# Five-layer graph network: later, pinned maxima over two blocks' totals, an earlier end of the early sums, and a reordered last tile

## The chip, the cores and the metric

The kernel runs on one core of one Trainium2 chip. The metric is the device time of one execution in microseconds (us); lower is better.

## The reference

A block with a normalised input and a graph network over N = 6250 nodes and E = 100000 edges, sorted by destination. The destinations are skewed: low node numbers have many edges.

```python
h = jnp.maximum(_layernorm(x, axis=-1), 0.0)           # x: 6250 x 256
h = _sage_mean(h, src, dst, n, deg, W1_self, W1_neigh, b1)            # 512 wide
h = _sage_pool(h, src, dst, n, deg, W2_pool, b2_pool, W2_self, W2_neigh, b2)
h = _sage_gcn(h, src, dst, n, deg, W3_neigh, b3)
h = _sage_mean(h, src, dst, n, deg, W4_self, W4_neigh, b4)
return x + (h @ W_fc + b_fc)

def _sage_pool(h, src, dst, n, deg, W_pool, b_pool, W_self, W_neigh, b):
    hp = jax.nn.relu(h @ W_pool + b_pool)
    hmax = jax.ops.segment_max(hp[src], dst, num_segments=n)
    hmax = jnp.where(deg[:, None] > 0, hmax, 0.0)
    return h @ W_self + hmax @ W_neigh + b
```

`_sage_mean` takes the mean over the incoming edges instead of the maximum, `_sage_gcn` a sum with the node itself divided by the degree plus one. The change lies in the second layer, the one with the maximum.

## The kernel before

Nodes are cut into 49 tiles of 128. Layer 1 ends with `hp` in DRAM (`tab_p`, the head of `rows2`) and the transposed inputs of each tile in `tab_t`. Layer 3 begins with the table `tab_r`, which layer 2 writes tile by tile, as three bf16 pieces of a float32 value.

**Layer 2's walk.** The edges are cut into six blocks of 52, 100, 220, 180, 130 and 100 steps (782 in all; a step is 128 edges, one for each partition), walked from the last block to the first. Each step issues one indirect gather on GpSimd (L1574) of 128 rows of `hp` into a row tile `X` (six tiles of two steps each), and the vector engine keeps a running maximum along each partition's edges with `step` (L1555), three instructions for two steps. Every second step the running rows go back to DRAM (L1559) into the block's own region of `rows2`. When a block is through, `carry` handles runs that go on from one partition to the next: four transposes (L1361), scans (L1369) and products (L1373), transposes back (L1391 or L1379), a maximum with the stored row (L1394), and a store.

**The tiles.** A tile's maximum is then one gathered row of one block ("total", tile `tot`, L1450), or of two blocks if its edges lie on both sides of a boundary. Tiles 37, 36, 24, 23, 11, 10 and 1 have two totals, tile 0 has its own routine, and the others one. `done2(d)` is a generator that issues the totals' gathers and the load of `th`, lets some steps pass (`yield`), takes the maximum of two totals (L1465), transposes it (L1469, L1472), multiplies (L1476, L1479 and L1482, float32), and rounds the result into three bf16 pieces (L1490 to L1498, each piece subtracted from the sum again by a product with minus the identity). At most one tile is begun every 11 steps (7 in the first block), from the highest to the lowest. `last_done2(0)` does the same for tile 0 after the last carry. The pool for `tot` and `th2` has four buffers of each.

**The early sums.** Part of layer 3 is done ahead: for the 16 destination tiles with the most edges, `early_products` multiplies blocks of the edge-count matrix (`ae`, loaded at L1526) with the rounded pieces of tiles 6 to 37, in batches of four source tiles (L562 and L564, 12 bf16 products or a few more for each destination tile and batch, into one of two PSUM banks `pd`), and `add3` adds each result to an accumulator on the vector engine (L1286). A batch is recorded when its last tile is rounded. `early.advance` (L1611) paces the recorded work.

**Order.** The program records instructions in this order, and a planner then sorts each engine's queue by its own costs and due times, within the dependencies. What is wrapped in `tc.keep_in_program_order` keeps its place among the so marked instructions. On the chip each queue runs in the planned order.

Of the kernel before, what the change touches and what calls it, by code (L numbers as in the profile page):

```python
# [15 lines left out]
ALU = mybir.AluOpType  # L16
# [4 lines left out]
P = 128  # L21
# [56 lines left out]
def fast_path(  # L78
# [15 lines left out]
    nc = tc.nc  # L94
# [8 lines left out]
    T = (E + P - 1) // P  # L103
    EP = T * P
    KI = FI // P
# [98 lines left out]
    ident = const.tile([P, P], F32, name="identf")  # L204
# [30 lines left out]
    at = 0  # L235
# [1055 lines left out]
    with tc.tile_pool(name="fl2c", bufs=1) as ck, ExitStack() as late:  # L1291
# [5 lines left out]
        usA = ck.tile([P, KI, FH], F32, name="usA")  # L1297
# [112 lines left out]
        def last_done2(d):  # L1410
            tots = [total(d, b) for b in range(1, b_of[d][1] + 1)]
            th = wk.tile([P, 2 * KI, P], F32, name="th2", bufs=4)
            nc.scalar.dma_start(th, tab_t[d].rearrange("p (k n) -> p k n", n=P))
            while not carried:
                yield
            tots.append(total(d, 0))
            pc = bank(psm, "pm", "pc_last")
            nc.tensor.matmul(pc, takes[d], carried[0], start=True, stop=True)
            pm = bank(psb, "pb", "pm_last")
            for k in range(2 * KI):  # L1420
                us = usA[:, k, :] if k < KI else usB[:, k - KI, :]
                product = nc.tensor.matmul(pm, th[:, k, :], us, start=(k == 0), stop=False)
                if k == 0:
                    tc.keep_in_program_order(product)
            hm = tots[0]
            nc.vector.tensor_tensor(hm, hm, pc, op=ALU.max)
            for t in tots[1:]:
                nc.vector.tensor_tensor(hm, hm, t, op=ALU.max)
            pt = bank(pst, "pt", "pt_hTf", (KH, P))
            for j in range(KH):  # L1430
                nc.tensor.transpose(pt[:, j, :], hm[:, j * P : (j + 1) * P], ident)
            hT = wk.tile([P, KH, P], F32, name="hTf")
            nc.scalar.copy(hT, pt)
            for c in range(KH):
                nc.tensor.matmul(pm, hT[:, c, :], un[:, c, :], start=False, stop=(c == KH - 1))
            r3 = early_pool[0].tile([P, 3 * FH], BF16, name="r3", bufs=2 * BATCH + 1)
            for part in range(3):
                piece = r3[:, part * FH : (part + 1) * FH]
                nc.scalar.copy(piece, pm)
                if part < 2:  # L1440
                    nc.tensor.matmul(pm, minus_b, piece, start=False, stop=True,
                                     skip_group_check=True)
            nc.scalar.dma_start(tab_r[d * P : (d + 1) * P, :], r3)
            yield
# [13 lines left out]

        def done2(d):
            tots, th = totals(d)  # L1460
            for _ in range(6):
                yield
            hm = tots[0]
            for t in tots[1:]:
                nc.vector.tensor_tensor(hm, hm, t, op=ALU.max)  # L1465
            yield
            pt = bank(pst, "pt", "pt_hTf", (KH, P))
            for j in range(KH):
                nc.tensor.transpose(pt[:, j, :], hm[:, j * P : (j + 1) * P], ident)  # L1469
            yield  # L1470
            hT = wk.tile([P, KH, P], F32, name="hTf")
            nc.scalar.copy(hT, pt)  # L1472
            yield
            pm = bank(psm, "pm", "pm_prf")
            for k in range(KI):
                nc.tensor.matmul(pm, th[:, k, :], usA[:, k, :], start=(k == 0), stop=False)  # L1476
            yield
            for k in range(KI):
                nc.tensor.matmul(pm, th[:, KI + k, :], usB[:, k, :], start=False, stop=False)  # L1479
            yield  # L1480
            for c in range(KH):
                nc.tensor.matmul(pm, hT[:, c, :], un[:, c, :], start=False, stop=(c == KH - 1))  # L1482
                if c == 1:
                    yield
            yield
            yield
            yield
            r3 = early_pool[0].tile([P, 3 * FH], BF16, name="r3", bufs=2 * BATCH + 1)
            hi, mid, lo = (r3[:, i * FH : (i + 1) * FH] for i in range(3))
            nc.scalar.copy(hi, pm)  # L1490
            yield
            nc.tensor.matmul(pm, minus_b, hi, start=False, stop=True, skip_group_check=True)
            yield
            nc.scalar.copy(mid, pm)
            yield
            nc.tensor.matmul(pm, minus_b, mid, start=False, stop=True, skip_group_check=True)
            yield
            nc.scalar.copy(lo, pm)  # L1498
            nc.scalar.dma_start(tab_r[d * P : (d + 1) * P, :], r3)
            if EARLY[0] <= d < EARLY[1]:  # L1500
                ready.append((d, r3))
                if len(ready) == BATCH or d == EARLY[0]:
                    early_products()
            yield
# [61 lines left out]
        for b in reversed(range(NB)):  # L1566
# [3 lines left out]
            for s0 in range(0, tb, G2):  # L1570
                X = (xmore if at // G2 % 2 else xpool).tile([P, G2, FH], F32, name="X2")
                for k in range(G2):
                    t = t0 + s0 + k
                    nc.gpsimd.indirect_dma_start(  # L1574
                        out=X[:, k, :], out_offset=None, in_=tab_p,
                        in_offset=bass.IndirectOffsetOnAxis(ap=srcI[:, t : t + 1], axis=0),
                    )
                    row, st = X[:, k, :], same[:, t : t + 1]
                    if s0 + G2 >= tb:
                        step(row, X[:, 0, :] if k else run, st, row)  # L1580
                        if k:
                            stored(b, s0 // 2, X)
                    elif k == 0 and s0:
                        step(run, run, st, row)
                    elif k:
                        held = run if s0 else X[:, 0, :]
                        if s0 == 0:
                            step(run, held, st, row)
                        step(X[:, 0, :], row, st, held)
                        if s0:  # L1590
                            step(run, run, st, row)
                        stored(b, s0 // 2, X[:, :1, :])
                    at += 1
                    if at > 8:
                        next(steps, None)
                        if todo and next(todo[0], 0) == 0:
                            todo.pop(0)
                    if at >= 130 and at % 12 == 0:
                        next(finding, None)
                    if at == MADE_AT:  # L1600
                        for _ in steps:
                            pass
                        top.close()
                        early_pool.append(
                            top.enter_context(tc.tile_pool(name="early3", bufs=1)))
                    if at <= EARLY_AT:
                        hub.advance(math.ceil(len(first) * max(0, at - 16) / (EARLY_AT - 16)))
                    else:
                        hub.advance(len(first) + math.ceil(
                            len(rest) * (at - EARLY_AT) / (T - 100 - EARLY_AT)))  # L1610
                    early.advance(early.done + math.ceil(  # L1611
                        early.left() / max(1, min(32, T - 16 - at))))
                    if b == 0 and s0 == 0 and k == 0:
                        for _ in finding:
                            pass
                    if b == 0 and not tiles and not ends and last_tiles and at >= T - 14:
                        now += [last_done2(d) for d in last_tiles]
                        last_tiles.clear()
                    if s0 + k > 2 and ends and next(ends[0], 0) == 0:
                        ends.pop(0)  # L1620
                        tiles += [d for d in reversed(range(NT)) if b_of[d][0] == last_b]
                    if (tiles and not (b and ends) and at >= begun_at + (11 if b else 7)
                            and begun2 < NT * (at - FIRST_AT) / (T - 36 - FIRST_AT)):
                        begun_at = at
                        now.append(done2(tiles.pop(0)))
                        begun2 += 1
                    for g in list(now):
                        if next(g, 0) == 0:
                            now.remove(g)
# [788 lines left out]
```

## Time and profile before

| | |
|---|---|
| median of 3 runs | 2730.45 us (2728.73 to 2737.01) |
| profiled execution | 2726.43 us, span 2724.6 us |
| mean granted TensorE clock | 0.944 |
| PE, DVE, ACT, POOL busy | 87%, 76%, 33%, 71% of the span |
| first and last gather of layer 2's walk | 721.4 us, 1815.2 us |

Times in the views are microseconds from the span's start. A group row has the line, engine, operation, tiles and shapes, the count, then the busy time and the mean of one in ns, then the engine's idle time ahead of these instructions and what ended it. A timeline row has the start, the length, the engine, the line, and in brackets the idle time ahead of it and its releaser. PE is TensorE's matmuls, PEld its weight loads, DVE the vector engine, ACT the scalar engine, POOL GpSimd, SP the queue of direct DMAs. The share of busy time is an average over stages that differ; the change is in the stage from 727 to some 1848 us.

### The profile page before, as it was taken

The numbers are of one execution on the slowest core, as the hardware profiler recorded it, in microseconds if no ns is written. First come the engines' busy times: TensorE is split into PE (matmuls) and PEld (weight loads), VectorE is DVE, ScalarE is ACT, GpSimd is POOL, SyncE is SP. The second block draws the span as 40 slices with busy tenths as digits, with TensorE's granted clock in tenths as the row PEclk, the third lists the DMA queues.
The fourth block names the chain that finished last, engine by engine and source line by source line (L and its number), as shares of the span: only waits on it lengthen the run. The fifth ranks groups of instructions, "written<-read, shape, count | busy, mean of one in ns | idle before, by whom it ended". The sixth has DMA issues, their size and how long they took to land.

```text
span 2724.6 us, 39212 instructions
## 1 busy us (share of the span) xinstructions
PE 2368.6 (87%) x11542; PEld 1282.5 (47%) x11674; DVE 2076.7 (76%) x5555; ACT 904.5 (33%) x2190; POOL 1938.3 (71%) x2266
## 2 busy tenths in 40 slices
PE   4698999999786675989899939986999999999998
PEld 2356667677443332434344414442444444565554
DVE  8898777766699798889789988972767766466665
ACT  5567767764388777212111111110000101000000
POOL 6477777777577777777677777745777775677776
PEclk8799999999897887999899969998999999999999
DMA  9467677777799999999999999979999998888886
GB/s 288 150 185 206 206 211 216 217 230 221 245 377 354 337 362 362 345 359 352 312 351 356 348 336 344 348 243 351 379 378 393 386 363 309 248 239 240 238 247 200
DMA packets 352251, 805.91 MB, mean 296 GB/s; under 512 B 56174, under 2 KB 150870, under 8 KB 351996
## 3 DMA queue, kind: packets, MB, share of 16 engines
q0 software_dynamic: 146080, 513.79, 57.3%
q1 hardware_dynamic: 139368, 206.78, 20.9%
q10 hardware_dynamic: 66580, 82.73, 8.9%
q8 instruction: 95, 1.56, 0.2%
q14 instruction: 128, 1.05, 0.1%
HBM read 604.99 MB, written 198.91 MB: 295 GB/s over the span
## 4 chain that ended last, share of the span: by engine, by line
PE 47%; DMA 28%; DVE 12%; issue 6%; POOL 3%; ACT 1%; ACTq 0%; SPq 0%; DVEq 0%; another core or an unknown queue 0%; POOLq 0%
PE pd L564 12%; PE pg L505 11%; DMA X<-rows,srcIf 11%; DVE run L1555 5%; PE pd L556 4%; DMA rows<-X 4%; DMA ring<-tab_h,srcT 4%; PE pm_hp L1157 3%; DVE X L1555 3%; DMA ring<-tab_s,srcE 2%; PE pd L557 2%; POOL X L1574 2%; PE pm_hp L1154 2%; PE pb L346 2%; PE pg L500 2%
## 5 line engine op out<-in xcount | busy, mean ns | idle before, releaser
L1574 POOL DMA_INDIRECT X<-rows,srcIf x782 | 742.5, 950 | 276.3 <-issue 146.4
L1555 DVE SCALAR_TENSOR_TENSOR run<-run,samef,X 128x512 f32<-128x512 f32 x758 | 571.0, 753 | 42.3 <-DMA X<-rows,srcIf 37.1
L483 POOL DMA_INDIRECT ring<-tab_h,srcT x474 | 456.3, 963 | 148.9 <-issue 56.4
L505 PE MATMUL pg<-ring,hot 128*128 128x259 bf16 (+1 forms) x2432 | 512.1, 320 | 53.2 <-DMA ring<-tab_h,srcT 30.7
L534 DVE SCALAR_TENSOR_TENSOR acc<-pg,M,acc 128x256 f32<-128x256 f32 (+2 forms) x694 | 356.3, 538 | 106.0 <-PE pg L505 76.8
L483 POOL DMA_INDIRECT ring<-tab_r,srcE x342 | 331.7, 970 | 133.5 <-issue 54.9
L564 PE MATMUL pd<-r,ae 128*128 128x512 bf16 x1492 | 372.6, 385 | 32.9 <-DVE acc L1286 30.3
L483 POOL DMA_INDIRECT ring<-tab_s,srcE x314 | 299.4, 954 | 117.5 <-PE pg L501 38.6
L505 PEld LDWEIGHTS <-hot 128*128 128x128 bf16 x2448 | 239.6, 98 | 257.8 <-issue 98.3
L1555 DVE SCALAR_TENSOR_TENSOR X<-X,samef,run 128x512 f32<-128x512 f32 x379 | 281.4, 742 | 43.0 <-DMA X<-rows,srcIf 13.1
L556 PE MATMUL pd<-zt,ac 128*128 128x512 bf16 x835 | 291.0, 382 | 7.1 <-DMA ac<-tab_a 5.5
L564 PEld LDWEIGHTS <-ae 128*128 128x128 fp8e4 x1536 | 151.6, 99 | 250.3 <-issue 110.1
L479 DVE TENSOR_SCALAR hot<-iota_bf,keyE 128x128 bf16<-128x128 bf16 x656 | 159.3, 267 | 115.1 <-PE pg L505 82.0
L557 PE MATMUL pd<-zt,ac 128*128 128x256 bf16 x882 | 241.6, 274 | 2.7 <-DVE zt L312 0.2
L564 PE MATMUL pd<-zt,ac 128*128 128x512 bf16 x797 | 221.8, 380 | 0.9
L1482 PE MATMUL pm_prf<-unf,hTf 128*128 128x512 f32 x384 | 187.8, 615 | 5.6 <-ACT hTf L1472 5.4
L564 PE MATMUL pd<-Z,A 128*128 128x256 bf16 (+1 forms) x1176 | 184.4, 274 | 0.7 <-ACT A L351 0.6
L338 ACT ACTIVATE hs<-ht,onef 128x128 bf16<-128x128 bf16 x396 | 153.4, 393 | 90.2 <-PE pb L346 88.6
L346 PE MATMUL pb<-hm,hs 128*128 128x392 bf16 x461 | 146.3, 337 | 11.7 <-DVE hm L340 11.5
L337 ACT ACTIVATE ht<-iota_bf,sk 128x128 bf16<-128x128 bf16 x396 | 153.0, 398 | 8.3
L340 DVE TENSOR_SCALAR hm<-iota_w,mk 128x392 bf16<-128x392 f16 x461 | 149.7, 332 | 5.2 <-PE pb L346 4.7
L479 DVE TENSOR_SCALAR hot<-iota_bf,keyT 128x128 bf16<-128x128 bf16 x474 | 122.5, 267 | 40.6 <-PE pg L505 39.4
(381 smaller groups left out, 3498.9 us busy)
## 6 DMA issues: line engine op xcount, KB each, us to landing
rows<-X SPq DMA_DIRECT2D x385, 256.0 KB
tab_r<-r ACTq DMA_DIRECT2D x49, 384.0 KB
rows<-hpf SPq DMA_DIRECT2D x49, 256.0 KB
th<-tab_t ACTq DMA_DIRECT2D x49, 256.0 KB
X<-rows,srcIf POOLq DMA_INDIRECT x782
ac<-tab_a ACTq DMA_DIRECT2D x90, 112.0 KB
tab_t<-th SPq DMA_DIRECT2D x37, 256.0 KB
tab_h<-Z SPq DMA_DIRECT2D x16, 579.0 KB
```

Of the source, the lines that this page charges most:

```text
L338: nc.scalar.activation(hots[0], t, AF.Relu, bias=one, scale=-1.0)
L346: nc.tensor.matmul(hold[0], hots[0], hots[1], start=(k == 0), stop=(k == k_of[w] - 1))
L479: nc.vector.tensor_scalar(hot[j], iota_b, keyT[:, j - jb : j - jb + 1], None, op0=ALU.is_equal)
L483: nc.gpsimd.indirect_dma_start(out=ring[:, j % deep, :], out_offset=None, in_=table, in_offset=bass.IndirectOffsetOnAxis(ap=srcT[:, j - jb ...
L505: nc.tensor.matmul(pg[:, : F + c], hot[j], X[:, part * F : (part + 1) * F + c], start=(k == 0 and part == 2), stop=(k == n - 1 and part == 1),
L534: nc.vector.scalar_tensor_tensor(acc[d], half, m, acc[d], op0=ALU.mult, op1=ALU.add)
L556: nc.tensor.matmul(hold[0], a, z[:, : 2 * F], start=(s == ss[0]), stop=False)
L557: nc.tensor.matmul(hold[0][:, :F], a, z[:, 2 * F :], start=False, stop=(s == ss[-1]))
L564: nc.tensor.matmul(hold[0][:, : F + c], a, z[:, part * F : (part + 1) * F + c], start=(s == ss[0] and part == 2 and s != own), stop=(s == ...
L1482: nc.tensor.matmul(pm, hT[:, c, :], un[:, c, :], start=False, stop=(c == KH - 1))
L1555: nc.vector.scalar_tensor_tensor(put, held, st, row, op0=ALU.mult, op1=ALU.max)
L1574: nc.gpsimd.indirect_dma_start(out=X[:, k, :], out_offset=None, in_=tab_p, in_offset=bass.IndirectOffsetOnAxis(ap=srcI[:, t : t + 1], axis=0),
```

## The change

- In `done2`, a tile with two totals lets 11 steps pass instead of 6 before its maximum, and the maximum keeps its place in program order among the marked instructions.
- The deadline towards which the early sums are paced is 30 steps ahead of the walk's end instead of 16 (the divisor is at most 32, so it counts from step 720 on).
- In `last_done2`, the two products with `usB` come behind the transposes and the copy of the maximum instead of ahead of them, and these products and transposes keep their program order.

No instruction is added or removed.

```diff
@@ last_done2
             pm = bank(psb, "pb", "pm_last")
-            for k in range(2 * KI):
-                us = usA[:, k, :] if k < KI else usB[:, k - KI, :]
-                product = nc.tensor.matmul(pm, th[:, k, :], us, start=(k == 0), stop=False)
-                if k == 0:
-                    tc.keep_in_program_order(product)
+            for k in range(KI):
+                tc.keep_in_program_order(
+                    nc.tensor.matmul(pm, th[:, k, :], usA[:, k, :], start=(k == 0), stop=False))
             hm = tots[0]
             nc.vector.tensor_tensor(hm, hm, pc, op=ALU.max)
             for t in tots[1:]:
                 nc.vector.tensor_tensor(hm, hm, t, op=ALU.max)
             pt = bank(pst, "pt", "pt_hTf", (KH, P))
             for j in range(KH):
-                nc.tensor.transpose(pt[:, j, :], hm[:, j * P : (j + 1) * P], ident)
+                tc.keep_in_program_order(
+                    nc.tensor.transpose(pt[:, j, :], hm[:, j * P : (j + 1) * P], ident))
             hT = wk.tile([P, KH, P], F32, name="hTf")
             nc.scalar.copy(hT, pt)
+            for k in range(KI):
+                tc.keep_in_program_order(
+                    nc.tensor.matmul(pm, th[:, KI + k, :], usB[:, k, :], start=False, stop=False))
             for c in range(KH):
                 nc.tensor.matmul(pm, hT[:, c, :], un[:, c, :], start=False, stop=(c == KH - 1))
@@ done2
             tots, th = totals(d)
-            for _ in range(6):
+            for _ in range(6 if len(tots) == 1 else 11):
                 yield
             hm = tots[0]
             for t in tots[1:]:
-                nc.vector.tensor_tensor(hm, hm, t, op=ALU.max)
+                tc.keep_in_program_order(nc.vector.tensor_tensor(hm, hm, t, op=ALU.max))
             yield
@@ the walk
                     early.advance(early.done + math.ceil(
-                        early.left() / max(1, min(32, T - 16 - at))))
+                        early.left() / max(1, min(32, T - 30 - at))))
```

## The prediction

> **What bounds the kernel now.** I read the page first, for the stage that the change touches. Layer 2 walks 782 gather steps (L1574): two vector recurrences or three per pair of steps (L1555), and beside them, on TensorE, the tiles' products (L1469 to L1496) and the early sums (L564, each closed by a vector add at L1286).
>
> ```profile
> span 2724.6 us, 39212 instructions
> L1574 POOL DMA_INDIRECT X<-rows,srcIf x782 | 742.5, 950 | 276.3 <-issue 146.4
> ```
>
> Then the windows view, cut where TensorE's state changes. Columns are length, busy time of PE, PEld, DVE, ACT and POOL (with counts), the granted TensorE clock, the DMA share and GB/s.
>
> ```profile
> core 0: us, PE busy (x) PEld busy (x) DVE busy (x) ACT busy (x) POOL busy (x), PEclk, DMA share, GB/s
> 1090.00:1589.00 499.00, 466.67 (x1755) 216.78 (x1788) 444.07 (x791) 98.91 (x189) 365.97 (x387) 0.97 0.99 347
> 1589.00:1634.00 45.00, 3.29 (x11) 1.62 (x10) 33.33 (x59) 7.39 (x10) 33.01 (x36) 0.52 0.95 330
> 1634.00:1654.00 20.00, 20.00 (x53) 9.68 (x54) 15.76 (x23) 4.51 (x9) 14.85 (x16) 0.89 0.91 295
> 1654.00:1826.00 172.00, 159.50 (x593) 73.43 (x604) 150.04 (x225) 19.30 (x34) 118.51 (x126) 0.98 0.95 333
> ```
>
> TensorE stands still for 42 us before 1634 and is then busy 179.5 of 192 us until 1826. So the end of layer 2 goes by TensorE: a fixed load of 179.5 us that starts at 1634. The chain of waits says the same: from 1798 to 1826 it runs through L564, L1476, L1479 and L1482. What starts the load is in the waits (engine, line, waited for: total, times, longest) and the timelines of DVE and PE.
>
> ```profile
> PE pt_hTf L1469 <- DVE tot L1465: 16.5, 1, 16.5
> PE pd L564 <- DVE acc L1286: 10.0, 4, 5.3
> DVE tot L1465 <- DMA tot<-rows,rows_of: 25.3, 4, 7.6
> ```
>
> ```profile
> 1624.76 0.75 DVE L1555 SCALAR_TENSOR_TENSOR run<-run,samef,X 128x512 f32<-128x512 f32 x1
> 1633.08 0.69 DVE L1465 TENSOR_TENSOR tot<-tot 128x512 f32<-128x512 f32 x1 [7.57 <-DMA tot<-rows,rows_of]
> ...
> 1641.92 0.69 DVE L1465 TENSOR_TENSOR tot<-tot 128x512 f32<-128x512 f32 x1 [3.78 <-DMA tot<-rows,rows_of]
> ...
> 1660.48 0.75 DVE L1555 SCALAR_TENSOR_TENSOR X<-X,samef,run 128x512 f32<-128x512 f32 x1 [1.01 <-DMA X<-rows,srcIf]
> ```
>
> ```profile
> 1633.83 1.11 PE L1469 MATMUL pt_hTf<-identf,tot 128*128 128x128 f32 x4 [16.52 <-DVE tot L1465]
> 1634.74 3.62 PE L1476 MATMUL pm_prf<-usA,th 128*128 128x512 f32 x4
> 1638.15 2.03 PE L1479 MATMUL pm_prf<-usB,th 128*128 128x512 f32 x4
> ...
> 1643.46 0.60 PE L1469 MATMUL pt_hTf<-identf,tot 128*128 128x128 f32 x4
> 1651.19 0.60 PE L1469 MATMUL pt_hTf<-identf,tot 128*128 128x128 f32 x4
> 1654.64 1.67 PE L564 MATMUL pd<-r,ae 128*128 128x512 bf16 x6
> ```
>
> Tile 11's maximum (L1465) starts the load: its four transposes at 1633.83 end TensorE's rest. Tile 10 follows at 1643.46, tile 9 at 1651.19, and the first early sum at 1654.64, as soon as tile 10 is rounded. The vector engine loses 7.57 and 3.78 us there, and the gathers hardly notice.
>
> **Edit 1: two-block maxima five steps later, pinned.** It concerns tiles 37, 36, 24, 23, 11, 10 and 1. In the built program, counting the recurrences L1555 in the vector queue, tile 11's maximum stood behind the 960th and now stands behind the 984th; tile 10's behind the 966th, now the 1000th. TensorE's queue holds nothing between the previous block's carry and tile 11's transposes in either program, so the rest before 1634 grows. By how much follows from GpSimd.
>
> ```profile
> 1627.53 0.95 POOL L1450 DMA_INDIRECT tot<-rows,rows_of  x1 [0.30 <-issue]
> ...
> 1645.04 0.95 POOL L1450 DMA_INDIRECT tot<-rows,rows_of  x1 [0.30 <-DVE run L1555]
> ...
> 1647.54 0.95 POOL L1574 DMA_INDIRECT X<-rows,srcIf  x1 [0.30 <-issue]
> ...
> 1654.37 0.95 POOL L1574 DMA_INDIRECT X<-rows,srcIf  x1 [0.30 <-issue]
> ...
> 1660.62 0.94 POOL L1450 DMA_INDIRECT tot<-rows,rows_of  x1 [0.30 <-issue]
> ...
> 1664.37 0.95 POOL L1574 DMA_INDIRECT X<-rows,srcIf  x1 [0.30 <-issue]
> ...
> 1684.38 0.95 POOL L1450 DMA_INDIRECT tot<-rows,rows_of  x1 [0.30 <-DMA rows<-X]
> ...
> 1685.63 0.94 POOL L1574 DMA_INDIRECT X<-rows,srcIf  x1 [0.30 <-issue]
> ```
>
> One gather takes 0.95 + 0.30 = 1.25 us of GpSimd. A row that the vector engine had to wait for, at 1660.48, was issued at 1654.37: 6.1 us from issue to use. The 983rd and 984th recurrence use the gather issued at 1647.54 (step 662). Ahead of it stood seven tile-total gathers (1627.53 the first, 1645.04 the seventh). The later maxima hold four "tot" buffers longer, and the pool has four, so tile 9's gather moves from step 658 to 672, and 8, 7 and 6 follow by 16 to 22 steps: only four are left ahead. Three fewer, 3 × 1.25 = 3.75, bring the gather to 1643.8, its use to 1649.9, the end of two recurrences of 0.75 to 1651.4, and the transposes, 0.75 behind the maximum's start as at 1633.08 and 1633.83, to 1652.1. That is **+18.3 us** for the start of the load, although the vector engine's waits of 7.57 and 3.78 go away.
>
> What is late next: tile 10's maximum, behind the 1000th recurrence, uses the gather issued at 1664.37; nine total gathers stood ahead of it (1660.62 the ninth), now five, so 4 × 1.25 earlier: 1659.4, used at 1665.5, + 0.75 for the recurrence and + 0.75 to the transposes: 1667.0. Tile 11's own chain lasts 1643.46 − 1633.83 = 9.6 us with its half-speed start, to 1661.7. TensorE rests **5.3 us**. Tiles 10 and 9 take 1651.19 − 1643.46 = 7.7 each, to 1682.4; tile 10's rounding ends 1654.64 − 1643.46 = 11.2 after its transposes, at 1678.2, and hides behind them. Two groups of early sums follow, into the two PSUM banks:
>
> ```profile
> 1811.20 2.59 PE pd L564 x12
> ```
>
> 2 × 2.6 brings TensorE to 1687.6. The third group needs the first one's add, which the vector queue now has behind the 1024th recurrence, whose gather was issued at 1685.63 behind ten total gathers (1684.38 the tenth), now eight: 1685.63 − 2.5 + 6.1 + 0.75 + 0.7 for the add = 1690.7, so **3.1 us** more of rest. Of the 179.5 us, 9.6 + 15.4 + 5.2 = 30.2 are then done, 149.3 are left: 1840.0.
>
> The remaining rests between 1654 and 1826 were 172 − 159.5 = 12.5. The largest hung on tile 1's maximum:
>
> ```profile
> 1792.98 0.69 DVE L1465 TENSOR_TENSOR tot<-tot 128x512 f32<-128x512 f32 x1 [7.40 <-DMA tot<-rows,rows_of]
> 1798.81 2.69 PE L564 MATMUL pd<-r,ae 128*128 128x512 bf16 x6 [5.35 <-DVE acc L1286]
> ```
>
> The wait of 7.40 blocked the add that L564 needed. It goes from that place: **−5.35**. Of the other 7.1 I keep 5, since TensorE comes later and finds more adds done (bounds 0, and all 12.5). TensorE gets to the last carry's transposes (L1361) at 1845.0, against 1826.1 (the first row under edit 3): **+18.9**.
>
> Nothing is cheap to cover here: the 42 us of rest before 1634 hid everything as long as the load started on time; with TensorE full behind it, each microsecond of a later start is a microsecond of the end.
>
> **Upstream of 1627** the pinned maxima of tiles 24 and 23 change a wait of 25.3 − 7.57 − 3.78 − 7.40 = 6.6 us. Their gathers are queued eight steps later too, behind a carry's store, so most of the wait stays; tiles 37 and 36 did not wait. I take −2 (bounds −5 and 0).
>
> **Edit 2: early sums to end 14 steps sooner.** The deadline can only pull forward what is already recorded. The last 16 groups are recorded when tile 6 is finished, and its gather goes from step 664 to 684. As built, the first of the last 32 adds stands behind recurrence 1024 (990 before), and four adds instead of one stand behind recurrence 1160, the last but one. So it brings nothing: 0, with the late sums already in the sum above.
>
> **Edit 3: the last tile's products around its transposes.**
>
> ```profile
> 1826.11 0.60 PE L1361 MATMUL ptcf<-identf,X 128*128 128x128 f32 x4
> ...
> 1832.82 0.69 DVE L1428 TENSOR_TENSOR tot<-tot 128x512 f32<-128x512 f32 x1
> ...
> 1834.15 1.88 PE L1422 MATMUL pm_last<-usB,th 128*128 128x512 f32 x4
> ...
> 1835.87 0.60 PE L1431 MATMUL pt_hTf<-identf,tot 128*128 128x128 f32 x4
> ...
> 1836.50 0.58 ACT L1433 COPY hTf<-pt_hTf 128x512 f32<-128x512 f32 x1 [6.57 <-PE pt_hTf L1431]
> 1837.14 3.70 PE L1435 MATMUL pm_last<-unf,hTf 128*128 128x512 f32 x8 [0.67 <-ACT hTf L1433]
> ```
>
> The maximum is ready at 1833.5, so the transposes can start at 1834.15 and the usB products cover the copy: the last products start 0.67 us sooner, all of it on the path: **−0.7** (0 if the maximum were later).
>
> **Behind layer 2** the loads of layer 3 wait for the last tile's store, so the shift passes on whole.
>
> ```profile
> 1844.59 2.22 DMA ac<-tab_a
> ...
> 1848.06 43.96 DMA zt<-tab_r
> ```
>
> **Sum.** +18.9 − 2 − 0.7 = +16.2 us on the profiled execution's 2726.4 us: 2742.6. The median of the runs is 2730.45, 4.0 above that execution, so 2746.7, rounded to **2747**. Lower bound: upstream −5, a rest of only 4 us between tiles 11 and 10 (16 recurrences at 0.75 us are 12, less 8 of work), no other rest: 1652.1 − 5 + 179.5 + 4 = 1830.6, +4.5 − 0.7 = +4. Upper: no upstream gain, rests of 5.3 + 3.1 + 12.5: 1852.5, +26.
>
> [...] The rows: in 1589:1634 the granted clock was 0.52, and tile 11's first four-matmul group took 3.62 us where the next took 2.03. [...]
>
> **Rivals.** (a) *Gathers set the end, faster.* If TensorE were done before the last recurrence, the removed waits would count: 7.57 + 3.78 + 7.40 = 18.75 us of vector idling. Of this GpSimd saw little; the tile totals moved behind the last gather free 3 × 1.25 = 3.75, and tile 1's wait at most 5.35 more: −9, less 0.7, about 2721. It decides if TensorE's queue is empty when the last recurrence ends. For: the vector engine is the one that waits. Against: 179.5 us of work in 192, and a start that is moved by 18 us. (b) *The change hardly shows*: TensorE closes its rests and upstream gains 5 or more: 0 to +8, 2730 to 2738. For: 12.5 us of rest exist. Against: the two new rests. (c) *Tile 1 makes a second stall.* Its gathers now follow the last step's gather and wait for block 1's carry store, and its pinned maximum stands ahead of the 1161st recurrence, the next-to-last early adds and the last carry. If its landing comes 6 us after TensorE needs those adds, the end is +22 and more, 2753 to 2759.
>
> **Numbers.** Forecast (2738.6 to 2753) 0.62; (c) 0.13; (b) 0.18; (a) 0.07. About 0.3%, 8.2 us, is what a measurement can tell from no change, so slower 0.75, same 0.18, faster 0.07. The range leaves out (a), the lower part of (b) and the tail of (c): 2731 to 2758.
>
> **What would show it.** Tile 11's transposes at about 1650 with a wait for DVE of some 33 us ahead of them, instead of 16.5; no wait of L1465 for its totals at tiles 11 and 10; a rest of about 5 us before tile 10's transposes; TensorE then full to the last carry's transposes, at about 1843; the last products 0.7 us sooner after them. It is wrong if those transposes come before 1640, or if the last carry's transposes wait for a recurrence rather than for TensorE's own queue.

## The result and the profile after

The changed kernel takes 2752.01 us (median of 5 runs, 2746.98 to 2753.65), the kernel before on the same chip 2734.47 us (5 runs, 2728.73 to 2737.01). The ratio is 1.0066, 95% interval 1.0048 to 1.0083: 18 us slower (13 to 23). The prediction had 16.2 us.

The page of the changed kernel's profiled execution (2753.65 us); lines of `done2` and the walk are two higher than before (L1467, L1471, L1576):

```profile
span 2751.8 us, 39207 instructions
L1576 POOL DMA_INDIRECT X<-rows,srcIf x782 | 744.0, 951 | 280.0 <-issue 144.2
```

The gathers cost what they did. The windows view of both kernels, cut at tile 11's transposes and at the last carry's transposes; first before, then after:

```profile
core 0: us, PE busy (x) PEld busy (x) DVE busy (x) ACT busy (x) POOL busy (x), PEclk, DMA share, GB/s
1633.80:1826.10 192.30, 179.77 (x645) 83.32 (x658) 166.00 (x248) 23.81 (x42) 133.56 (x141) 0.97 0.95 329
```

```profile
core 0: us, PE busy (x) PEld busy (x) DVE busy (x) ACT busy (x) POOL busy (x), PEclk, DMA share, GB/s
1661.40:1855.30 193.90, 180.32 (x645) 83.23 (x657) 149.46 (x225) 23.35 (x41) 121.86 (x128) 0.97 0.87 300
```

The count of matmuls is the same, 645, and they take 180 us in both, in a stretch that is only 1.6 us longer, but which starts 27.6 us later in this pair of profiles. The waits of the changed kernel from 1589 to 1860, and the timelines of DVE and PE at tiles 11 and 10 and at the third group of early sums:

```profile
PE pt_hTf L1471 <- DVE tot L1467: 37.4, 2, 34.4
PE pd L564 <- DVE acc L1286: 8.6, 5, 3.2
```

```profile
1660.74 0.68 DVE L1467 TENSOR_TENSOR tot<-tot 128x512 f32<-128x512 f32 x1
...
1676.03 0.68 DVE L1467 TENSOR_TENSOR tot<-tot 128x512 f32<-128x512 f32 x1
...
1832.55 0.69 DVE L1467 TENSOR_TENSOR tot<-tot 128x512 f32<-128x512 f32 x1 [3.24 <-DMA tot<-rows,rows_of]
...
1855.96 0.73 DVE L1369 TENSOR_TENSOR_SCAN segf<-keepTf,ptcf 128x128 f32<-128x128 f32 x2 [14.79 <-PE ptcf L1361]
```

```profile
1661.48 1.11 PE L1471 MATMUL pt_hTf<-identf,tot 128*128 128x128 f32 x4 [34.42 <-DVE tot L1467]
...
1676.86 0.63 PE L1471 MATMUL pt_hTf<-identf,tot 128*128 128x128 f32 x4 [2.96 <-DVE tot L1467]
1677.32 3.54 PE L1478 MATMUL pm_prf<-usA,th 128*128 128x512 f32 x4
...
1700.93 1.46 PE L564 MATMUL pd<-r,ae 128*128 128x512 bf16 x6 [1.75 <-DVE acc L1286]
```

The first two maxima no longer wait for their totals; TensorE waits for them, 34.42 instead of 16.52 us, and then again for tile 10. The last row of DVE shows what the end waits for: the vector engine stands 14.79 us for the last carry's transposes. Its last recurrence ends 21.4 us ahead of them (at 1833.9, the transposes start at 1855.32); in before these were only 2.6 us (1823.5 and 1826.11). In the chain of waits the shift passes on behind the last tile, as it did before:

```profile
1875.13 42.36 DMA zt<-tab_r
```

Not all of the 27.6 us is the change's. The medians differ by 18 us only, and the profiled execution of before took 2726.43 us, where the five runs have 2728.73 to 2737.01. The carry ahead of tile 11 is 9.5 us late already, and it is as late in the run `e1_1` below, which up to there has the queues of the kernel before. The timelines of PE, before, after and `e1_1`:

```profile
1603.48 1.11 PE L1361 MATMUL ptcf<-identf,X 128*128 128x128 f32 x4 [14.37 <-DVE X L1555]
```

```profile
1613.00 1.11 PE L1361 MATMUL ptcf<-identf,X 128*128 128x128 f32 x4 [3.60 <-DVE X L1557]
```

```profile
1613.45 1.11 PE L1361 MATMUL ptcf<-identf,X 128*128 128x128 f32 x4 [14.38 <-DVE X L1557]
```

So one profiled execution differs from another by up to 10 us upstream. Counted from this carry, tile 11's transposes moved from 30.35 to 48.48 us, by 18.1, and the last carry's from 222.6 to 242.3, by 19.7. That is the part of the shift that arises behind this carry, and it is close to the 18 us of the medians. Whether a few microseconds ahead of the carry belong to the change as well stays open: from the walk's first gather to this carry it is 882.0 us in before and 887.9 us in the changed kernel, 885.6 to 889.8 in the five other traces with eleven steps and the pin for tiles 24 and 23, and 882.6 to 884.7 in five without them; but `e1_1` has 891.5 without them, and the time of `e1_up`, which has them alone, shows no loss (0.0 us, -3.3 to 3.3).

### The profile page after: what moved, and what is told of

Same layout as the page of the kernel before. It is cut to its first block, busy times and chain, and to the rows that moved or that the text cites. A ratio compares the mean times of both kernels' runs of the same rounds, so it can differ in the third digit from the quotient of the medians.

```text
span 2751.8 us, 39207 instructions
## 1 busy us (share of the span) xinstructions
PE 2366.7 (86%) x11543; PEld 1279.5 (46%) x11674; DVE 2081.8 (76%) x5555; ACT 906.4 (33%) x2190; POOL 1941.8 (71%) x2266
## 5 line engine op out<-in xcount | busy, mean ns | idle before, releaser
L1576 POOL DMA_INDIRECT X<-rows,srcIf x782 | 744.0, 951 | 280.0 <-issue 144.2
```

The costliest lines, as they stand in the source:

```text
L1576: nc.gpsimd.indirect_dma_start(out=X[:, k, :], out_offset=None, in_=tab_p, in_offset=bass.IndirectOffsetOnAxis(ap=srcI[:, t : t + 1], axis=0),
```

## The experiments

"Us" is the measured ratio less one, times the median of before in the same group (2731.74 to 2734.47 us). "Behind" gives the recurrences ahead of the maxima of tiles 11, 10 and 1 in the vector queue, as built.

| run | what is changed in before | behind | ratio (95%) | us |
|---|---|---|---|---|
| after | all three edits | 984, 1000, 1160 | 1.0066 (1.0048, 1.0083) | +18.0 |
| e1_1110 | edit 1, tiles 11 and 10 | 984, 1000, 1148 | 1.0086 (1.0071, 1.0101) | +23.5 |
| e1_rest | edit 1, the other five tiles | 960, 963, 1132 | 0.9981 (0.9971, 0.9991) | -5.2 |
| e1_1 | edit 1, tile 1 | 960, 966, 1132 | 0.9978 (0.9965, 0.9992) | -6.0 |
| e1_up | edit 1, tiles 37, 36, 24, 23 | 960, 963, 1125 | 1.0000 (0.9988, 1.0012) | 0.0 |
| e1_pin6 | pin only, six steps | 976, 993, 1161 | 1.0038 (1.0024, 1.0053) | +10.4 |
| pin11_10 | edit 1, tile 10 | 960, 1000, 1151 | 1.0084 (1.0066, 1.0103) | +23.0 |
| e23 | edits 2 and 3 | 960, 966, 1135 | 0.9996 (0.9984, 1.0008) | -1.1 |
| best | all but tiles 11 and 10 | 960, 963, 1135 | 1.0007 (0.9995, 1.0019) | +1.9 |
| lead2 | `best`, products moved ahead | 960, 963, 1132 | 1.0001 (0.9989, 1.0013) | +0.3 |
| lead_1 | `e1_1`, products moved ahead | 960, 966, 1132 | 0.9972 (0.9961, 0.9983) | -7.7 |
| before_light | 8 groups of early sums left out | 960, 966, 1112 | 0.9987 (0.9972, 1.0002) | -3.6 |
| after_light | the same in the changed kernel | 984, 1000, 1143 | 1.0017 (1.0004, 1.0030) | +4.6 |

### Which tiles: e1_1110 and e1_rest

```diff
-            for _ in range(6):
+            for _ in range(11 if d in (11, 10) else 6):
...
-                nc.vector.tensor_tensor(hm, hm, t, op=ALU.max)
+                op = nc.vector.tensor_tensor(hm, hm, t, op=ALU.max)
+                if d in (11, 10):
+                    tc.keep_in_program_order(op)
```

`e1_rest` is its complement: `11 if len(tots) == 2 and d not in (11, 10)`, pinned for `d not in (11, 10)`.

> The kernel before, with eleven steps and the pin for tiles 11 and 10 alone; tiles 37, 36, 24, 23 and 1, the deadline of the early sums and the last tile are as before. As built, the two maxima stand behind recurrences 984 and 1000, as in the changed kernel. Theory 'later start' (TensorE's fixed load behind tile 11 starts later, and each us of it is a us of the end): +17 to +20 us on before, tile 11's transposes 18 us later after the carry of its block, as in the changed kernel. Rival 'upstream' (the changed kernel's profile is 9.5 us late at the previous block's carry already, so half of the loss arises among tiles 37 to 23): +8 to +10. Rival 'tail' (tile 1's maximum and the earlier deadline make the loss): 0 to +5.

> The kernel before, with eleven steps and the pin for tiles 37, 36, 24, 23 and 1, but not for 11 and 10; the rest as before. As built, tile 11's maximum stays behind recurrence 960, tile 1's goes from 1125 to 1132. 'Later start': -5 to +1 us (a wait of some 5 us upstream goes). 'Upstream': +8 to +10, with the previous block's carry 9.5 us later than before. 'Tail': +5 to +10 by tile 1's maximum.

Measured +23.5 (19 to 28) and -5.2 us (-8 to -2.5); together +18.3, which is the changed kernel. That rules out "upstream" and "tail". "Later start" named the right place, but the size in the expectation (17 to 20) was too small: it carried the gain of tile 1's wait into a run that leaves tile 1 as it was. The wait is there, 7.10 us at the vector engine, and TensorE's rest of 5.55 us behind it, in PE's timeline of `e1_1110`:

```profile
1652.60 1.12 PE L1471 MATMUL pt_hTf<-identf,tot 128*128 128x128 f32 x4 [33.61 <-DVE tot L1465]
...
1667.95 1.09 PE L1471 MATMUL pt_hTf<-identf,tot 128*128 128x128 f32 x4 [4.20 <-DVE tot L1465]
...
1823.99 1.44 PE L564 MATMUL pd<-r,ae 128*128 128x512 bf16 x3 [5.55 <-DVE acc L1286]
```

The prediction's terms without tile 1 give 18.9 + 5.35 = 24.3 us, and the measurement is 23.5.

### Start or second tile: pin11_10

The diff is that of `e1_1110` with `d == 10` in place of `d in (11, 10)`.

> The kernel before, with eleven steps and the pin for tile 10 alone. As built, tile 11's maximum stays behind recurrence 960 and tile 10's goes from 966 to 1000; TensorE's queue still has tile 11, then 10, then 9. Theory 'the later of the two waits' (TensorE's load behind tile 10's transposes sets the end; the four us that TensorE rested before them in the run with tiles 11 and 10 say that tile 10's maximum decided there): tile 11's transposes as before, then a rest of some 20 us before tile 10's, and +20 to +26 us, as with both tiles. Rival 'the start alone' (only tile 11's transposes count, what follows closes up): 0 to +6 us.

Measured +23.0 us (18 to 28). PE's timeline:

```profile
1636.48 1.12 PE L1471 MATMUL pt_hTf<-identf,tot 128*128 128x128 f32 x4 [16.88 <-DVE tot L1465]
...
1670.07 1.08 PE L1471 MATMUL pt_hTf<-identf,tot 128*128 128x128 f32 x4 [21.89 <-DVE tot L1465]
```

TensorE starts as in before, with a wait of 16.88, does tile 11, and then stands for 21.89 us in front of tile 10. The whole loss is there although the start did not move. (A later maximum of tile 11 alone was not run.) So "the load starts later at tile 11" is too narrow: what counts is the last wait before TensorE's queue runs through, and in the changed kernel that is tile 10's maximum behind recurrence 1000.

### Pin or steps: e1_pin6

```diff
             for _ in range(6):
                 yield
...
-                nc.vector.tensor_tensor(hm, hm, t, op=ALU.max)
+                tc.keep_in_program_order(nc.vector.tensor_tensor(hm, hm, t, op=ALU.max))
```

> The kernel before, with the pin for all two-block maxima, but six steps as before; deadline and last tile as before. As built, tile 11's maximum stands behind recurrence 976 and tile 10's behind 993 (before 960 and 966, changed 984 and 1000): 8 recurrences, 5.3 steps of 1.25 us of GpSimd, less than in the changed kernel. 'Later start': 18.3 - 6.7 = +11.6 us for tile 11's transposes, tile 10's 5.8 us sooner than there, so that +11 to +14 us of the time is made by the pin alone, and only some 5 by the five steps. If instead the five steps make it, 0 to +3. 'Upstream' (37 to 23 stand behind 397, 413, 648 and 665, partly later than in the changed kernel): +9 or more with the delay seen at the previous block's carry.

Measured +10.4 us (7 to 14.5), just below the 11 to 14 expected. From the carry, tile 11's transposes stand at 40.7 us, 10.4 later than before, and tile 10's 17.1 later, where the changed kernel has 23.9. By the medians, more than half of the 18.0 us is the pin's. The positions as built say how: without the pin the planner puts the maxima of tiles 11 and 10 behind recurrences 960 and 966, with it they stay later, behind 976 and 993. With eleven steps and no pin, the built queue has them behind 960 and 966, as before (not run), so without the pin the five steps would not move these two at all. Why the planner chooses that place was not looked into.

### The other tiles: e1_1 and e1_up

> The kernel before, with eleven steps and the pin for tile 1 alone. As built, its maximum goes from behind recurrence 1125 to 1132; everything else up to there stands as before. Theory A (the 5.2 us that the five other tiles gained together come from tile 1, whose wait of 7.4 us kept an early add and with it TensorE 5.35 us from its work): -3 to -6 us. Theory B (they come from tiles 37, 36, 24 and 23): 0, within 1.5 us.

> The kernel before, with eleven steps and the pin for tiles 37, 36, 24 and 23 alone. As built, their maxima go from behind 386, 397, 633 and 636 to 398, 404, 647 and 656; tile 11's stays behind 960, tile 1's behind 1125. Theory A (tile 1 made the gain): 0, or up to +3, since in the profile with both changes the last carry but two came 5.8 us later after the first gather than before. Theory B (these four made it): -3 to -6 us. The prediction's step had -2 (-5 to 0).

`e1_1` is the diff of `e1_1110` with `d == 1`, `e1_up` with `d in (37, 36, 24, 23)`. Measured -6.0 us (-9.6 to -2.2) and 0.0 (-3.3 to 3.3). Theory A holds: tile 1 made the gain, and the four upstream tiles none that shows within 3.3 us. DVE's timeline of `e1_1`, in place of before's wait of 7.40:

```profile
1807.25 0.69 DVE L1465 TENSOR_TENSOR tot<-tot 128x512 f32<-128x512 f32 x1 [2.25 <-DMA tot<-rows,rows_of]
```

TensorE has no rest of over 0.5 us left there. Seven recurrences (1125 to 1132) were enough. The wait stood ahead of the last recurrences too, and it is 5.15 us shorter; how much of the gain comes by TensorE's add and how much by them was not run apart.

### The rest of the change: e23 and best

The diffs are those of edits 2 and 3 and of `e1_rest` above.

> The kernel before, with the deadline of the early sums at 30 steps and the last tile's products around its transposes; all maxima of two blocks as before. As built, the adds of the last early sums end behind recurrence 1145 instead of 1161. 'Later start': -0.7 us by the last tile, and up to -3 if the earlier sums leave TensorE's queue emptier when the last carry comes. 'Upstream': the same. 'Tail': +5 to +10 by the deadline.

> The changed kernel without its edit for tiles 11 and 10: eleven steps and the pin for 37, 36, 24, 23 and 1, the deadline at 30 steps, the last tile's products around its transposes. If the parts add up: -5.2 - 0.4 = -5.6 us on before (-4 to -8). If the earlier early sums have already taken what tile 1's pin gains: 0 to -2.

Measured -1.1 us (-4.4 to 2.2) and +1.9 us (-1.4 to 5.2), neither clear of no change. The second expectation failed: the parts do not add up. DVE's and PE's timelines of `best` show two reasons:

```profile
1806.03 0.69 DVE L1467 TENSOR_TENSOR tot<-tot 128x512 f32<-128x512 f32 x1 [7.72 <-DMA tot<-rows,rows_of]
...
1837.08 0.69 DVE L1426 TENSOR_TENSOR tot<-tot 128x512 f32<-128x512 f32 x1 [2.25 <-DMA tot<-rows,rows_of]
```

```profile
1808.82 1.44 PE L564 MATMUL pd<-r,ae 128*128 128x512 bf16 x3 [4.33 <-DVE acc L1286]
...
1837.83 1.11 PE L1430 MATMUL pt_hTf<-identf,tot 128*128 128x128 f32 x4 [2.01 <-DVE tot L1426]
1838.73 3.14 PE L1435 MATMUL pm_last<-usB,th 128*128 128x512 f32 x4
```

First, tile 1's wait is back, 7.72 us, with TensorE's rest of 4.33: as built, edit 2 moves tile 1's gathers from behind step 764 to 770, and the maximum only from 1132 to 1135. At 1.5 recurrences a step the maximum stands 20 recurrences ahead of its gathers' place again (1135 against 1155), as before (1125 against 1146, 21), and not 14 as in `e1_1` (1132 against 1146). `e23`, without the pin, has it behind 1135 too, and there it waits 8.31 us. Second, where TensorE is not late, tile 0's total is: its maximum waits 2.25 us for it. With edit 3 TensorE then has nothing in hand, rests 2.01 us, and runs the `usB` products behind the transposes in 3.14 us. How the two share the loss was not run apart.

### Is it TensorE's load: after_light, before_light, lead2, lead_1

The light runs leave out half of the last batch:

```diff
-            for d in range(H3):
+            for d in range(H3 if ss[0] != EARLY[0] else H3 // 2):
```

> The changed kernel without the early sums of the last batch of source tiles for eight of the sixteen destination tiles: 8 groups of 12 products and 8 adds are left out, so layer 3's result lacks them. 8 x 2.6 = 21 us of TensorE's load go from the stage behind tile 11's maximum. Theory 'TensorE's load sets the end': -15 to -21 us on the changed kernel, so -3 to +3 us on before, until the last recurrence sets the end. Rival (the end goes by the recurrences and their gathers, TensorE's lateness only accompanies it): within 3 us of the changed kernel, +15 to +20 us on before.

> The kernel before without the same 8 groups of early sums. Theory: before is only some 3 to 8 us of load above the point where the last recurrence sets the end (with 5.6 us less load the last carry waited 3.1 us for a recurrence), so -3 to -8 us on before, although 21 us of load go; and the distance between the changed kernel and before shrinks from 18 us to 3 to 8 us. If TensorE's load sets the end throughout: -15 to -21 us on before, and the distance stays 18 us.

The changed kernel without 21 us of load is at +4.6 us (1 to 8), so it gave back 13 of its 18; before gave back 3.6 (-0.5 to 8). The distance between the two shrank from 18 to 8.2 us, just above the 3 to 8 expected. Waits of PE in `before_light`, and of PE and DVE in `after_light`:

```profile
PE ptcf L1361 <- DVE X L1555: 23.5, 2, 20.9
```

```profile
PE ptcf L1361 <- DVE X L1557: 3.8, 1, 3.8
```

```profile
1825.27 0.69 DVE L1467 TENSOR_TENSOR tot<-tot 128x512 f32<-128x512 f32 x1 [8.71 <-DMA tot<-rows,rows_of]
```

In before, the 21 us that were taken out turned into a rest of 20.9 us ahead of the last carry's transposes: the last recurrence came no sooner (219.6 us after the carry ahead of tile 11, against 219.3). In `after_light`, too, the last carry waits for a recurrence, which is why it did not give back the 15 us or more that were expected. There tile 1's maximum waits 8.7 us for its totals just ahead of the last recurrences, after which the vector engine works without a rest up to the last one; that this wait makes the remaining 8 us was not run apart. Its trace suggests that TensorE's lateness is behind it as well: the second of these totals hangs on the carry of the block before, whose transposes start at 1778.50, 23.8 us after the last recurrence of that block ended, while in `before_light` they wait 2.52 us for that recurrence. So before stood at the point where load and recurrences end together, which is why a later maximum costs nearly its full length and a shorter load brings next to nothing.

What TensorE can do sooner was tried as well. In `lead2` and `lead_1` the products that need no maximum are recorded ahead of it:

```diff
             tots, th = totals(d)
+            lead = d in (11, 10)
+            if lead:
+                pm = bank(psm, "pm", "pm_prf")
+                for k in range(2 * KI):
+                    us = usA[:, k, :] if k < KI else usB[:, k - KI, :]
+                    nc.tensor.matmul(pm, th[:, k, :], us, start=(k == 0), stop=False)
```

> The kernel of the run above, with the products of tiles 11 and 10 with usA and usB recorded ahead of their maxima. As built, tile 11's eight products now stand ahead of its transposes, in TensorE's rest before its maximum; tile 10's stay behind tile 11's transposes. Theory 'later start' (TensorE's load behind tile 11's maximum sets the end): 3.6 + 2.0 = 5.6 us leave the load, so 4 to 6 us less than the run above, some -10 us on before. Rival 'gathers' (once the load is a little lighter the gathers set the end): no more than 1 us less than the run above. Rival 'carry' (the products stand among the carry's transposes back, delay its store and with it tile 11's total): 0 to 4 us more than the run above, with tile 11's transposes that much later.

> The kernel before, with eleven steps and the pin for tile 1 alone (measured at -5.9 us), and the products of tiles 11 and 10 with usA and usB recorded ahead of their maxima, of which tile 11's land in TensorE's rest. Theory 'gathers' (with tile 1's wait gone and 5.6 us less load the last recurrence sets the end): -6 to -9 us on before, at most 3 us less than tile 1's pin alone. Theory 'load': -10 to -13 us.

`lead2` is 1.6 us below `best`, with intervals that overlap, and its last carry waits 3.06 us for a recurrence (rival "gathers"). `lead_1` is at -7.7 us (-10.7 to -4.6), 1.7 below `e1_1`, which again overlaps; its last carry waits 1.62 us for a recurrence:

```profile
1822.31 0.66 PE L1361 MATMUL ptcf<-identf,X 128*128 128x128 f32 x4 [1.62 <-DVE X L1565]
```

Both `e1_1` and `lead_1` beat the kernel before and the changed one. The gain is tile 1's pin; that the products moved ahead add to it is not shown.

## Why the prediction was right

**What bounds the kernel: right, in one direction.** A fixed load of 180 us behind the maxima is shown by the windows and by `pin11_10`. The last carry's transposes at 1855.32 (row below) have no wait ahead of them: they come when TensorE's queue gets to them. The prediction saw that a later start costs its full length. It did not say how near the other bound was: `before_light` puts it 3.6 us below.

**Tile 11's start, +18.3: right.** Counted from the carry ahead of it +18.1. The wait of 34.42 was predicted as some 33.

**Rest before tile 10's transposes, 5.3: right in size.** 2.96, with two waits of 0.67 for the roundings, 4.3 in all; tile 10's transposes came 15.4 us behind tile 11's, predicted 14.9. The prediction told this rest as an addition to the start. `pin11_10` shows it the other way round: tile 10's maximum alone makes the whole loss.

**Rest at the third group, 3.1:** 1.75. **All rests** of the stretch: 193.90 - 180.32 = 13.6 us, predicted 5.3 + 3.1 + 5 = 13.4.

**Tile 1, -5.35: right.** `e1_1` measured -6.0, with a smaller move (1132, not 1160). In the changed kernel its maximum still waits 3.24 us, but the rest of TensorE that followed it is gone, and rival (c) with it.

**Upstream, -2: mis-sized.** `e1_up` measured 0.0 (-3.3 to 3.3). The wait that was to shrink, at tile 24, grew: 6.58 us in before, 8.83 in `e1_up`, 9.36 in the changed kernel. Without this term the sum is 18.2 us, nearer to the 18.0 measured.

**Edit 2, 0: right for the changed kernel, not in general.** `e1_1110`, `e1_rest` and the changed kernel add up without a term for it. With tiles 11 and 10 as before, it brings tile 1's wait back.

**Edit 3, -0.7: right in sign for the changed kernel alone.** From the last carry's transposes to the last products it took 1864.23 - 1855.32 = 8.9 us, before 1837.14 - 1826.11 = 11.0. Of these 2.1 us the covered copy is 0.67, the term that was predicted. Another 0.9 is the product `pc_last` (1.13 us, before 2.07) and 0.6 the `usA` products (1.88 us, before 2.46), for which the granted clock was 0.62 in before (1830 to 1834) and 1.00 in the changed kernel (1859 to 1863): the sum did not have this, and it is luck. In `best` the same order took 1841.71 - 1828.96 = 12.75. The prediction's "0 if the maximum were later" was the step that failed: with a later maximum the `usB` products no longer fill that wait, and come behind it. PE's timeline of the changed kernel:

```profile
1855.32 0.60 PE L1361 MATMUL ptcf<-identf,X 128*128 128x128 f32 x4
...
1859.39 1.13 PE L1418 MATMUL pc_last<-fixf,takes 128*128 128x512 f32 x2 [0.87 <-ACT fixf L1380]
1860.35 1.88 PE L1422 MATMUL pm_last<-usA,th 128*128 128x512 f32 x4
1862.07 0.61 PE L1430 MATMUL pt_hTf<-identf,tot 128*128 128x128 f32 x4
1862.52 1.88 PE L1435 MATMUL pm_last<-usB,th 128*128 128x512 f32 x4
1864.23 1.02 PE L1437 MATMUL pm_last<-unf,hTf 128*128 128x512 f32 x2
```

**Tile 10's products: slower than in the sum.** The sum took 7.7 us for tile 10, its length in before, where no rest came ahead of it. Behind the rest of 2.96 us in the changed kernel its `usA` products took 3.54 us, at a granted clock of 0.54 (1677.3 to 1681), where such a group takes 1.88 us at 1.00 (the row at 1860.35 above): 1.7 us more. The third group's rest was 1.4 us smaller than predicted, which fits with most of the 1.7 us being hidden there.

## What to carry to other kernels

Moving an instruction back in its queue can remove the wait ahead of it, but it also delays everything that needs its result. So look at both: who needs the result, and whom the wait holds up. Here TensorE stood idle for the maxima of tiles 11 and 10, and moving them back to save the vector engine 7.57 and 3.78 us of waiting cost 23.5 us. At tile 1 a like wait of 7.40 us blocked an add that TensorE needed, and moving that one maximum back by seven recurrences gained 6 us. TensorE's load and the recurrences ended together in the kernel before, and a step that made the load later cost nearly in full (18.0 us for 18.1), while one that made it shorter gained little (3.6 us for 21).

## What was not expected of the hardware

Behind short stretches of light work TensorE's granted clock was lower in some runs and not in others. In `best`, ahead of the `usB` products that took 3.14 us, TensorE had worked 1.82 of 3.80 us, with a single rest of 2.01 us. The windows view:

```profile
core 0: us, PE busy (x) PEld busy (x) DVE busy (x) ACT busy (x) POOL busy (x), PEclk, DMA share, GB/s
1834.00:1837.80 3.80, 1.82 (x5) 0.51 (x3) 1.38 (x2) 0.00 (x0) 0.14 (x1) 1.00 0.30 69
1837.80:1841.70 3.90, 3.87 (x8) 2.11 (x9) 0.00 (x0) 0.59 (x1) 0.00 (x0) 0.56 0.00 0
```

The granted clock was 1.00 in the first of these stretches and 0.56 in the second. In before it was 0.62 from 1830 to 1834, where no rest in the 4 us ahead was longer than 0.68 us, and `pc_last` took 2.07 us; in the changed kernel, with the same order of small pieces ahead of it, it was 1.00 from 1859 to 1863 and `pc_last` took 1.13. Nor did the longer rest go with the slower products. In `e23`, at the place of the rest of 2.01 us in `best`, TensorE rested 2.71 us, and its `usB` products then took 1.88 us, not 3.14:

```profile
1841.57 0.65 PE L1430 MATMUL pt_hTf<-identf,tot 128*128 128x128 f32 x4 [2.71 <-DVE tot L1426]
1842.06 1.88 PE L1435 MATMUL pm_last<-usB,th 128*128 128x512 f32 x4
```

What decides between two such stretches was not shown.
